# Sixteen full pages of a routed feed-forward are worked on between the norms and the routing of the last quarter of tokens

## The chip, the cores and the metric

The kernel runs on one core of a Trainium2 chip. The core has five engines with a queue of instructions each: TensorE (PE in the profile; PEld are its weight loads), VectorE (DVE), ScalarE (ACT), GpSimd (POOL) and SyncE (SP), which mostly issues transfers. Each engine works through its own instructions in the order in which the program gives them, and waits for semaphores where it needs what another engine or a transfer makes. The metric is device time in microseconds (us); lower is better. The runs of the kernel before took 815.91 us in the median (812.72, 815.91, 818.84).

## What is computed

The input x has 8 sequences of 256 tokens with 256 numbers each, 2,048 tokens, all in 32-bit floating point. One layer is computed:

```python
x = x + attention(layernorm(x))
x = x + ffn(layernorm(x))
```

The attention is differential: 16 heads with two sets of queries and keys of 8 numbers, two softmaxes, and their difference weighted by a scalar lambda, then a root-mean-square norm of each head's 16 numbers and a product with wo:

```python
attn = attn1 - lambda_full * attn2
rms = rsqrt(mean(attn * attn, axis=-1) + 1e-5)
attn = (attn * rms * subln_w * (1 - LAMBDA_INIT)).reshape(b, t, 256) @ wo.T
```

The feed-forward is a mixture of experts. A gate gives each token 32 logits; the four largest are chosen and weighted by a softmax over those four:

```python
logits = x @ gate_w.T
sel = top_k(sigmoid(logits), 4)
w = softmax(logits)[sel]; w = w / w.sum()
```

There are 32 large experts (256 to 96 to 256) and 16 small ones (256 to 128 to 256); two neighbouring large experts share a small one. Each token goes through its four large experts and the small ones that belong to them:

```python
a = silu(x @ Wg[e]) * (x @ Wu[e]) * w        # likewise with cWg, cWu of e // 2
y += a @ Wd[e]                               # likewise 0.05 * (a_small @ cWd[e // 2])
```

## The kernel before, in words

**Quarters and steps.** The tokens are worked on in four quarters of 512 (`NIT` = 4, index `it`). Attention of a quarter has four steps, one for each group of four heads, so there are sixteen steps `s`. Scores, exponentials, products with the values and the running maxima of the next step are interleaved by hand (`both`, `values`, `normalize`). What belongs to the end of a quarter (`epilogue`: norm of the heads, product with wo, layer norm, then `route`) is a Python generator that yields after each small group of instructions; `fill` takes one piece after another of it in between the attention of the next quarter. So the order on TensorE, ScalarE, VectorE and SP is that in which the program issues its instructions (`manual_schedule`, `MANUAL`), and Pool's order is left to the planner.

**Pages.** `route` (L543) gives each of a token's four choices a row in a page. A page (`pages` in device memory) has 128 rows of 304 numbers and belongs to one expert; a row holds the normed token, its 32 weights and its token number. When an expert's page is full, it gets the next free number. The state that goes from quarter to quarter is small: `held` (pages of each expert so far), `given` (pages given out, a running sum), `shift_of`, `count` and `chosen` (the expert of each page, one page per partition). The rows are written by indirect transfers of Pool, one for each choice and 128 tokens (L671, "puts"): 16 in a quarter.

**The last quarter.** No attention is left to hide its epilogue. It is cut into two halves of 256 tokens (`halves`, made at the end of the attention's block), which the loop under `with ExitStack() as last` (L848) takes in turns, one piece of each. The norms' roots (`rsqrt`, L249) are Ln and Exp on ScalarE with one refining step on VectorE. At the end of the second half's routing, `tables` (L688) makes for every page the offsets of its expert's weights (`table`, read into TensorE's registers) and the expert's number (`expert`). The gate and up weights of the small experts, `ws_sb`, are loaded at the start of this stretch in four transfers of 1 MB (L840), since they take the room of attention's buffers.

**The pages' work.** `run_tiles` works on 84 pages (`OFTEN`); up to 11 more follow if the routing gave out more. A page goes through five stages, which are staggered: `fetch` (L868: SP loads page i, seven pages ahead, eight buffers), `turn` (L872: token numbers and weights are copied or picked out on VectorE, two transposes on TensorE, the copy `xTe` on VectorE), `up` (L889: eight matrix products `gu` for gate and up of the large and the small expert, Silu on ScalarE, the product `act` on VectorE), `turn_act` (L921: two transposes, two copies `aTe`) and `down` (L930: the products `dn`, their scaling by the weight on ScalarE, and an indirect transfer on Pool that adds the rows to a sum in device memory, L943). Even pages add to one sum, odd pages to another, and two adds to one sum never overlap. The first sum also holds the attention's result of each quarter (L536). At the end both sums are read, added and written out.

Of the kernel before, what the change touches and what calls it, by code (L numbers as in the profile page):

```python
# [33 lines left out]
OFTEN = 84  # L34
RW = 304
# [4 lines left out]
def kernel(  # L40
# [171 lines left out]
    )  # L212

# [17 lines left out]
    with actx:  # L231
# [17 lines left out]
        def rsqrt(dst, v, tag):  # L249

            y = r2.tile(list(v.shape), F32, tag=f"{tag[0]}ry", name=f"ry_{tag}")
            nc.scalar.activation(y, v, AF.Ln)
            nc.scalar.activation(y, y, AF.Exp, scale=-0.5)
            yield "any"
            t = r2.tile(list(v.shape), F32, tag=f"{tag[0]}rt", name=f"rt_{tag}")
            nc.vector.scalar_tensor_tensor(t, y, -0.5, y, ALU.mult, ALU.mult)
            nc.vector.tensor_tensor(t, t, v, ALU.mult)
            nc.vector.scalar_tensor_tensor(dst, t, 1.5, y, ALU.add, ALU.mult)

        def layernorm_T(src, dst, tag, rows=None, n=NA):  # L260
# [12 lines left out]
            yield from rsqrt(rs, ve, f"n{tag}")  # L273
# [225 lines left out]
        def epilogue(it, a0=0, n=NA):  # L499
# [19 lines left out]
            yield from rsqrt(rms, ms, f"h{tag}")  # L519
# [16 lines left out]
            nc.sync.dma_start(out=sums_dram[0][ts].rearrange("(a p) e -> p a e", p=P), in_=xt)  # L536
            x2 = turned("x2T", tag, n, hidden)
            yield from layernorm_T(xt, x2, f"f{tag}", rowsrc[:, a0 : a0 + n, 0:E], n)
# [4 lines left out]
        def route(it, x2, a0, n):  # L543
# [13 lines left out]
            if a0 == 0:  # L557
                t = choice[it] = {
                    name: r1.tile([P, NA, w], F32, tag=name, name=f"{name}_{it}")
                    for name, w in (  # L560
                        ("lg", NE), ("top", 8), ("ex", NE), ("eq", NE), ("key", 8), ("mask", NE),
                        ("slots", NE), ("slot", 8), ("wsum", 1),
# [51 lines left out]
            slots, slot = t["slots"], t["slot"]  # L614
            nc.vector.tensor_copy(slots, pos.rearrange("p (a e) -> p a e", e=NE))
            nc.vector.tensor_scalar(whole, whole, 7, None, ALU.logical_shift_right)
# [50 lines left out]
            for a in range(n):  # L667
                if it + 1 < NIT:
                    yield "any"
                for k4 in range(TOPK):  # L670
# [9 lines left out]
                    tc.add_to_no_dep_group("puts", put.ins)  # L680
                if it + 1 < NIT:
                    yield "wait"
            if m + n == NIT * NA:
                tables()
# [3 lines left out]
        def tables():  # L688

            tiles = e1.tile([1, 1], I32)  # L690
            nc.vector.tensor_copy(tiles, given[0:1, (NIT + 1) % 2, NE - 1 : NE])
            found["tiles"] = tiles
            whose = e1.tile([P, 2], I32)
            nc.vector.tensor_copy(whose[:, 1:2], chosen)
            nc.vector.tensor_scalar(whose[:, 0:1], whose[:, 1:2], NE - 1, None, ALU.bitwise_and)
            nc.vector.tensor_scalar(whose[:, 1:2], whose[:, 0:1], 1, None, ALU.logical_shift_right)
            et = e1.tile([P, 5], F32)
            nc.vector.tensor_copy(et[:, 0:1], whose[:, 0:1])
            for i, (j, size) in enumerate(((0, INTER), (1, P), (0, E), (1, E))):
                nc.vector.tensor_scalar(  # L700
                    et[:, 1 + i : 2 + i], whose[:, j : j + 1], float(size), None, ALU.mult
                )
            rows = one("rows")
            for i in range(4):
                nc.tensor.transpose(
                    rows[0:1, i * P : (i + 1) * P], et[:, 1 + i : 2 + i], ident
                )
            table = e1.tile([1, P, 4], I32)
            nc.vector.tensor_copy(
                table.rearrange("p t i -> p i t"),  # L710
                rows[0:1, 0 : 4 * P].rearrange("p (i t) -> p i t", t=P),
            )

            diag = e1.tile([P, P], F32)
            nc.vector.tensor_scalar(diag, ident, et[:, 0:1], None, ALU.mult)
            by_row = one("by_row")[:, 0:P]
            nc.tensor.matmul(by_row, lhsT=ones, rhs=diag, start=True, stop=True)
            expert = e1.tile([P, P], F32)
            nc.vector.tensor_copy(expert, by_row)
            found["tables"] = (table, expert)  # L720
# [117 lines left out]
    for kc in range(2):  # L838
        for i, w in enumerate((cwg, cwu)):
            nc.sync.dma_start(out=ws_sb[:, kc, i, :], in_=w[kc * P : (kc + 1) * P, :])  # L840
    iota = e1.tile([P, P], F32)
    nc.gpsimd.iota(
        iota, [[1, P]], base=0, channel_multiplier=0, allow_small_or_imprecise_dtypes=True
    )
# [3 lines left out]
    with ExitStack() as last, tc.manual_schedule(engines=MANUAL):  # L848
        del psum["big"]
        psum_pools(last, "last", 0, 8)  # L850

        for _ in range(4):
            next(halves[0])
        while halves:
            for g in list(halves):
                if next(g, None) is None:
                    halves.remove(g)
            fill("any")
        while side:
            fill("pe", "any")  # L860

    table, expert = found["tables"]
    ps_e = xctx.enter_context(tc.tile_pool(name="ps_e", bufs=2, space=bass.MemoryType.PSUM))

    with tc.manual_schedule(engines={mybir.EngineType.PE, mybir.EngineType.Pool}):
        regs, xg, xT, act, aT, weight, token = {}, {}, {}, {}, {}, {}, {}

        def fetch(i):  # L868
            xg[i] = e2.tile([P, RW], F32, tag="xg", name=f"xg_{i}", bufs=8)
            nc.sync.dma_start(out=xg[i], in_=pages[i])  # L870

        def turn(i):  # L872

            token[i] = e2.tile([P, 1], I32, tag="token", name=f"token_{i}", bufs=10)
            nc.vector.tensor_copy(token[i], xg[i][:, RT : RT + 1].bitcast(I32))  # L875
# [170 lines left out]
```

## Time and profile before

| what | value |
| --- | --- |
| runs | 812.72, 815.91, 818.84 us |
| the profiled execution | 821.01 us, of which the span from first to last instruction is 818.8 |
| TensorE busy | 662.6 us (81% of the span), mean granted clock 0.882 |
| VectorE, ScalarE, Pool busy | 378.8, 276.8, 246.9 us |
| transfers | 83.58 MB, 102 GB/s in the mean |
| last attention product (TensorE) | ends near 470 us |
| first page fetched (SP) | 527.75 us |
| first and last add to the sums (Pool) | 542.45 and 790.56 us |

All positions are in us from the start of the span. A row of a timeline gives the start, the duration, the engine, the line of the kernel, the operation, what it writes and reads, how many instructions are merged, and in brackets how long the engine had been idle and what ended that. A row of the waits gives who waited for whom, the us in total, how often, and the longest. "issue" in the chain is time in which an engine waited for nothing that the profile shows, "remote" a wait for an event that it can't assign. The page's slices give busy shares in tenths, 9 for 90% or more.

### The profile page before, as it was taken

The page shows a single profiled execution, that of the slowest core. Times are in us where ns is not written, and L with a number is a line of the kernel's source. Part 1 is how long each engine was busy: PE and PEld are TensorE (multiplying, and loading weights), DVE is VectorE, ACT ScalarE, POOL GpSimd, SP SyncE. Part 2 cuts the span into 40 slices and gives each one's busy share as a digit, 9 for nine tenths or more (in the row PEclk, how much of TensorE's full clock was granted, in tenths as well). Part 3 has the DMA queues.
Part 4 walks back from the last instruction along what each step waited for, and adds up shares of the span by engine and source line. Part 5 has one row for each costly group of instructions (what it writes and reads, how often), then busy time and mean ns, then how long its engine had stood idle before and what let it go on. Part 6 is the DMA issues. An engine that isn't in the chain of part 4 may idle for free.

```text
span 818.8 us, 12293 instructions
## 1 busy us (share of the span) xinstructions
PE 662.6 (81%) x4108; PEld 428.5 (52%) x4108; DVE 378.8 (46%) x1111; ACT 276.8 (34%) x539; POOL 246.9 (30%) x246
## 2 busy tenths in 40 slices
PE   7789989899659998688886652199999999999930
PEld 6445434445224554233442242098888888888830
DVE  2274556555726666435654146243443344344312
ACT  2025545545215553234443311033223322332320
POOL 5000111111171110622105202524555455455540
PEclk7889999999868998878979665589999999999975
DMA  3107071714232334211461150445555555555347
GB/s 105 30 15 245 10 231 48 231 41 124 77 114 55 119 96 131 87 43 44 102 157 69 53 232 31 135 102 99 94 95 99 93 94 97 97 90 98 45 55 299
DMA packets 62512, 83.58 MB, mean 102 GB/s; under 512 B 8049, under 2 KB 54257, under 8 KB 61937
## 3 DMA queue, kind: packets, MB, share of 16 engines
q1 hardware_dynamic: 45488, 58.50, 23.5%
q0 software_dynamic: 15168, 20.98, 15.3%
q10 hardware_dynamic: 1792, 3.28, 1.3%
q8 instruction: 37, 0.61, 0.3%
q14 instruction: 27, 0.21, 0.1%
HBM read 36.23 MB, written 42.31 MB: 96 GB/s over the span
## 4 chain that ended last, share of the span: by engine, by line
PE 41%; DMA 22%; DVE 17%; issue 9%; ACT 5%; another core or an unknown queue 4%; SPq 1%; ACTq 0%; POOL 0%; DVEq 0%
DMA sums<-ye,token 18%; PE sm L411 9%; PE sc L395 8%; PE pv L448 7%; DVE mp L424 6%; PE gu L909 2%; PE wo L315 2%; PE po L467 2%; PE qps L352 2%; ACT ye L942 2%; PE vps L315 2%; DMA y<-sums 2%; DVE xTe L886 1%; DVE act L919 1%
## 5 line engine op out<-in xcount | busy, mean ns | idle before, releaser
L424 DVE TENSOR_REDUCE mp<-sm 128x4 f32<-128x1024 f32 x128 | 156.0, 1223 | 145.3 <-PE sm L411 127.2
L411 PE MATMUL sm<-kb,qT 32*128 32x512 f32 x512 | 159.5, 720 | 42.1 <-DVE mp L424 34.7
L421 ACT ACTIVATE pt<-sc 128x1024 f32<-128x1024 f32 x128 | 130.5, 1023 | 185.6 <-PE sm L411 149.5
L943 POOL DMA_INDIRECT sums<-ye,token x84 | 131.1, 1561 | 134.8 <-ACT act L918 106.8
L395 PE MATMUL sc<-qa,kb 32*128 32x256 f32 x1024 | 159.6, 437 | 11.4 <-ACT pt L421 6.5
L395 PEld LDWEIGHTS sc<-qa,kb 32*128 32x128 f32 x1024 | 88.0, 201 | 56.8 <-issue 32.9
L486 POOL TENSOR_SCALAR on<-on,nlam 128x128 f32<-128x128 f32 x28 | 17.0, 606 | 309.7 <-DVE on L474 286.9
L909 PE MATMUL gu<-ws_sb,xTe 128*128 x336 | 87.4, 383 | 0.0
L671 POOL DMA_INDIRECT pages<-rowsrc,index x64 | 62.7, 980 | 66.2 <-issue 52.8
L875 DVE COPY token<-xg 128x1 int32<-128x1 int32 x84 | 12.9, 154 | 150.7 <-DMA sums<-ye,token 136.3
L448 PE MATMUL pv<-pt,vaug 128*32 128x512 f32 x512 | 76.8, 671 | 5.5 <-ACT oT L457 5.5
L927 ACT ACTIVATE aTe<-at 128x128 f32<-128x128 f32 x84 | 23.3, 278 | 164.2 <-DVE aTe L926 164.1
L411 PEld LDWEIGHTS sm<-kb,qT 32*128 32x128 f32 x512 | 42.7, 204 | 61.0 <-DVE mp L424 50.2
L909 PE MATMUL gu<-wl_sb,xTe 128*128 x336 | 70.6, 333 | 0.6 <-DMA xg<-pages 0.6
L909 PEld LDWEIGHTS gu<-ws_sb,xTe 128*128 128x128 f32 x336 | 62.5, 193 | 4.5
L909 PEld LDWEIGHTS gu<-wl_sb,xTe 128*128 128x128 f32 x336 | 57.5, 192 | 8.6 <-issue 2.9
L933 PE MATMUL dn<-wdl_sb,aTe 96*128 x168 | 53.6, 401 | 0.0
L937 PE MATMUL dn<-wds_sb,aTe 128*128 x168 | 50.1, 379 | 0.0
L884 PE MATMUL xt<-ident,xg 128*128 128x128 f32 x168 | 32.7, 278 | 12.5 <-DMA xg<-pages 12.5
L942 ACT ACTIVATE ye<-dn,weight 128x256 f32<-128x256 f32 x84 | 39.4, 469 | 1.1 <-PE dn L937 1.0
L886 DVE COPY xTe<-xt 128x256 f32<-128x256 f32 x84 | 35.3, 420 | 8.2 <-PE xt L884 8.0
L448 PEld LDWEIGHTS pv<-pt,vaug 128*32 128x32 f32 x512 | 10.7, 113 | 50.7 <-issue 42.6
(178 smaller groups left out, 781.1 us busy)
## 6 DMA issues: line engine op xcount, KB each, us to landing
pages<-free SPq DMA_DIRECT2D x31, 456.0 KB
xg<-pages SPq DMA_DIRECT2D x84, 152.0 KB
wl_sb<-in_wg_dram SPq DMA_DIRECT2D x8, 384.0 KB
wl_sb<-in_wu_dram SPq DMA_DIRECT2D x8, 384.0 KB
wdl_sb<-in_wd_dram SPq DMA_DIRECT2D x8, 384.0 KB
x<-in_x_dram SPq DMA_DIRECT2D x4, 512.0 KB
kb<-packk SPq DMA_DIRECT2D x128, 16.0 KB
sums<-zero SPq DMA_DIRECT2D x8, 256.0 KB
```

What stands on the lines that cost most here:

```text
L395: nc.tensor.matmul(sc[:, j, h * 256 : h * 256 + 256], lhsT=kb[s][rows, h, c * P : (c + 1) * P], rhs=qa[s][rows, c // 2 * 256 : c // 2 * 25 ...
L411: nc.tensor.matmul(sm[:, j, :], lhsT=qT[m][rows, a * P : (a + 1) * P], rhs=kb[m][rows, :, ks], start=True, stop=True,)
L421: nc.scalar.activation(pt, sc, AF.Exp, scale=SM_SCALE)
L424: nc.vector.tensor_reduce(mps[m % 2][:, a, 2 * mp : 2 * mp + 2, 2 * D : 2 * D + 2], sm.rearrange("p j (s k) -> p j s k", s=2), AX.X, ALU.max,)
L448: nc.tensor.matmul(pv[s][32 * j : 32 * j + 32, :], lhsT=st_it[it][1][:, c, 4 * g + j, :], rhs=pts[(s, c, j // 2)][:, j % 2, :], start=(c % ...
L671: put = nc.gpsimd.indirect_dma_start(pages.rearrange("r s w -> (r s) w"), bass.IndirectOffsetOnAxis(ap=index[:, a, k4 : k4 + 1], axis=0), ...
L886: nc.vector.tensor_copy(xT[i], ps)
L909: nc.tensor.matmul(ps[:, :, cols], lhsT=xT[i][:, kc, :], rhs=w[:, kc, :, bass.ds(first, n)], start=(kc == 0), stop=(kc == 1),)
L933: nc.tensor.matmul(ps, lhsT=aT[i][0:INTER, 0], rhs=wdl[0:INTER, bass.ds(large, E)], start=True, stop=False,)
L937: nc.tensor.matmul(ps, lhsT=aT[i][:, 1], rhs=wds[:, bass.ds(small, E)], start=False, stop=True,)
L942: nc.scalar.activation(y, ps, AF.Copy, scale=weight.pop(i))
L943: nc.gpsimd.indirect_dma_start(sums_dram[i % 2], bass.IndirectOffsetOnAxis(ap=token.pop(i), axis=0), y, None, compute_op=ALU.add, oob_is_e ...
```

## The change

The quarters, the attention and the pages' work on a single page stay as they are. Changed is which pages are worked on when:

- After the routing of the third quarter, `full_first` marks the pages that are full by then (all of an expert's pages but its last, unless that one is full to the end). Ranks among the marked pages are found by a product with the triangular matrix `upper`; the first 16 (`FULL`) are put in order by a product with a one-hot matrix (`in_order`). No row of them is free for the last quarter, and none of their tokens is from it, so the program is told that their loads and adds don't depend on the last quarter's puts and stores.
- In the last quarter's loop each piece of a half is followed by two pieces of `run_tiles(0, FULL)`, which has become a generator; 16 pages are interleaved with the two halves there. The stretch has its own banks of PSUM: two for the transposes, two for gate and up, one for the down product, and three for the halves (before, the halves had eight).
- `rest_after` takes the place of `tables`: it orders the remaining pages in the same way after the last routing, and the pages from 16 on follow in the old place.
- Since the order of the pages is known only on chip, each `fetch` reads the page's number into a register of SP first.
- The roots of the last quarter (`by_bits`) are made on VectorE from the number's bits and three refining steps, eleven instructions, without Ln and Exp. ScalarE still has the routing's Exp, between the pages' Silu. For the first 16 pages ScalarE makes both `aTe` copies.
- `ws_sb` is loaded in 16 transfers of 256 KB, four columns of experts at a time; `iota` moves to the start of the kernel.

On Pool, the order in which the program is built is: adds of pages 0 to 10, the 8 puts of the first half, adds of pages 11 and 12, the 8 puts of the second half, adds of pages 13 to 15, then the rest. On SP the store of the first half's rows stands behind the 16 loads of `ws_sb` and ahead of page 0, that of the second half behind page 11.

The diff, cut to its core:

```diff
+FULL = 16
...
-        def rsqrt(dst, v, tag):
+        def rsqrt(dst, v, tag, by_bits=False):
             y = r2.tile(list(v.shape), F32, tag=f"{tag[0]}ry", name=f"ry_{tag}")
+            if by_bits:
+                t = r2.tile(list(v.shape), F32, tag=f"{tag[0]}rt", name=f"rt_{tag}")
+                nc.vector.tensor_scalar(
+                    t.bitcast(I32), v.bitcast(I32), 1, None, ALU.logical_shift_right
+                )
+                nc.vector.tensor_scalar(
+                    y.bitcast(I32), t.bitcast(I32), -1.0, float(0x5F3759DF), ALU.mult, ALU.add
+                )
+                for i in range(3):
+                    nc.vector.scalar_tensor_tensor(t, y, -0.5, y, ALU.mult, ALU.mult)
+                    nc.vector.tensor_tensor(t, t, v, ALU.mult)
+                    nc.vector.scalar_tensor_tensor(
+                        dst if i == 2 else y, t, 1.5, y, ALU.add, ALU.mult
+                    )
+                return
...
-            yield from rsqrt(rms, ms, f"h{tag}")
+            yield from rsqrt(rms, ms, f"h{tag}", not hidden)
...
-            yield from layernorm_T(xt, x2, f"f{tag}", rowsrc[:, a0 : a0 + n, 0:E], n)
+            yield from layernorm_T(xt, x2, f"f{tag}", rowsrc[:, a0 : a0 + n, 0:E], n, not hidden)
...
+            if it + 2 == NIT:
+                yield from full_first(k + 1, chosen_by)
             if m + n == NIT * NA:
-                tables()
+                yield "any"
+                yield from rest_after()
...
+        def in_order(pool, name, et, flags, rank, n):
+            at = pool.tile([P, n], F32, name=f"at_{name}")
+            nc.vector.tensor_scalar(at, iota[:, 0:n], rank, flags, ALU.is_equal, ALU.mult)
+            by = pool.tile([P, n], F32, name=f"by_{name}")
+            nc.vector.tensor_scalar(by, at, et[:, 0:1], None, ALU.mult)
+            yield "pe"
+            rows = one(f"rows_{name}")
+            for i in range(5):
+                nc.tensor.matmul(
+                    rows[0:1, i * n : (i + 1) * n], lhsT=et[:, 1 + i : 2 + i], rhs=at,
+                    start=True, stop=True,
+                )
...
+            yield "pe"
+            ps = one(f"expert_{name}")
+            nc.tensor.matmul(ps[:, 0:n], lhsT=ones, rhs=by, start=True, stop=True)
...
+        def rank_of(pool, name, flags):
+            ps = one(f"rank_{name}")
+            nc.tensor.matmul(ps[:, 0:1], lhsT=upper, rhs=flags, start=True, stop=True)
+            rank = pool.tile([P, 1], F32, name=f"rank_{name}")
+            nc.vector.tensor_copy(rank, ps[:, 0:1])
+            return rank
+
+        def full_first(k, chosen_by):
+            yield "any"
...
+            full = r1.tile([P, 1], F32, name="full")
+            nc.vector.tensor_scalar(full, given[:, k % 2, NE - 1 : NE], tok[:, 0:1], None, ALU.is_gt)
+            nc.vector.tensor_tensor(full, full, part, ALU.subtract)
+            et = whose_pages(r1, "full")
+            yield "pe"
+            rank = rank_of(r1, "full", full)
+            nc.vector.scalar_tensor_tensor(
+                in_full, rank, float(FULL), full, ALU.is_lt, ALU.mult
+            )
+            yield from in_order(r1, "full", et, in_full, rank, FULL)
...
+    def load_small(c):
+        cols = slice(c * P, (c + 4) * P)
+        for kc in range(2):
+            for i, w in enumerate((cwg, cwu)):
+                nc.sync.dma_start(out=ws_sb[:, kc, i, cols], in_=w[kc * P : (kc + 1) * P, cols])
...
+    def fetch(i):
+        table, j, first = place(i)
+        _, (at,) = nc.values_load_multi_w_load_instructions(
+            table[0:1, j, 4:5], engines={mybir.EngineType.SP},
...
+        load = nc.sync.dma_start(
+            out=xg[i], in_=pages[bass.ds(at, 1)].rearrange("one s w -> (one s) w")
+        )
+        if first:
+            tc.declare_no_dep(
+                load.ins, group="last puts", reason="no row of a full page is free"
+            )
+            tc.add_to_no_dep_group("full pages", load.ins)
...
-            nc.vector.tensor_copy(aT[i][0:INTER, 0], ps[0:INTER, 0])
+        (nc.scalar.copy if i < FULL else nc.vector.tensor_copy)(aT[i][0:INTER, 0], ps[0:INTER, 0])
...
-    with ExitStack() as last, tc.manual_schedule(engines=MANUAL):
+    with ExitStack() as gap, tc.manual_schedule(engines=MANUAL):
         del psum["big"]
-        psum_pools(last, "last", 0, 8)
+        psum["tiles"] = gap.enter_context(
+            tc.tile_pool(name="ps_full", bufs=2, space=bass.MemoryType.PSUM)
+        )
+        psum["tr"], psum["dn"] = 2, 1
+        psum_pools(gap, "gap", 0, 3)
+        load_small(0)
+        tiles = run_tiles(0, FULL)
         for _ in range(4):
             next(halves[0])
+        for c in range(4, NC_SMALL, 4):
+            load_small(c)
         while halves:
             for g in list(halves):
                 if next(g, None) is None:
                     halves.remove(g)
+                for _ in range(2):
+                    next(tiles, None)
             fill("any")
+        for _ in tiles:
+            pass
...
-        run_tiles(0, OFTEN)
+        for _ in run_tiles(FULL, OFTEN):
+            pass
```

## The prediction

> **What bounds the kernel now.** I read the page's slices first, then the chain of work that ended last, then the timeline of one engine after another around the stretch that the change fills. Three rows of the slices (20.5 us each; TensorE busy, its granted clock, DMA, in tenths):
>
> ```profile
> PE   7789989899659998688886652199999999999930
> PEclk7889999999868998878979665589999999999975
> DMA  3107071714232334211461150445555555555347
> ```
>
> Attention fills the left, the pages' work the right; between them TensorE falls to 2 and 1 tenths at half clock. The chain in order of time and Pool's and SP's timelines say what is there:
>
> ```profile
> 489.80 37.95 issue
> 529.55 2.24 DMA xg<-pages
> ...
> 764.26 3.89 DMA sums<-ye,token
> ```
>
> ```profile
> 505.73 0.99 POOL L671 DMA_INDIRECT pages<-rowsrc,index  x1 [35.65 <-issue]
> 507.02 0.96 POOL L671 DMA_INDIRECT pages<-rowsrc,index  x1 [0.30 <-issue]
> ...
> 525.26 0.96 POOL L671 DMA_INDIRECT pages<-rowsrc,index  x1 [0.30 <-issue]
> ```
>
> ```profile
> 472.44 0.35 SPq L840 DMA_DIRECT2D ws_sb<-in_cwg_dram  x1
> ...
> 527.75 2.23 SPq L870 DMA_DIRECT2D xg<-pages  x5
> ```
>
> From 470 to 527.75 the last quarter is normed and routed, and its 16 puts, 1.27 us apart on Pool, end it: the first page is fetched 2.49 us after the last put starts. Then 84 pages follow, and their rate is Pool's:
>
> ```profile
> 678.83 1.56 POOL L943 DMA_INDIRECT sums<-ye,token  x1 [1.11 <-ACT act L918]
> 682.30 1.56 POOL L943 DMA_INDIRECT sums<-ye,token  x1 [1.92 <-ACT act L918]
> 684.96 1.56 POOL L943 DMA_INDIRECT sums<-ye,token  x1 [1.10 <-ACT act L918]
> ```
>
> An add waits for the add before it on the same of two sums (678.83 to 684.96: 6.1 us a pair). First add 542.45, last 790.56, so 2.99 us a page, and 28.2 us after the last one. TensorE alone would need 2.82: from 540 to 560, before the adds hold it back, its gate and up groups start 2.82 us apart.
>
> **The change, part by part.**
>
> *Sixteen pages leave the last phase*: 16 x 2.99 = 47.8 us. There are always sixteen: 1,536 tokens times 4 rows are 6,144, 32 experts can leave at most 32 x 127 of them in short pages, so 2,080 remain, 17 pages at least. What counts is how late the 17th page is fetched against 527.75, since its fetch still waits for the last put. Break-even is a fetch at 575.5.
>
> *When the early pages start.* The small experts' weights are still loaded at 472.4, now in 16 pieces with rows of 2 KB instead of 8. The row of before moved 4.2 MB at 422 to 434 GB/s; the nearest row with shorter ones, wds_sb with 1 KB, 348. So 9.7 to 12 us; I take 10.5, landed at 485. Half 0's root is now 11 dependent VectorE steps of 0.22 (2.4 us) instead of two table steps and three: x is ready about 1.6 us later, at 482, SP stores it and only then issues page 0's fetch (it stands behind that store), which takes 2.2 us as at 529.9 and comes in behind the weights. Transposes and copy follow, and gate and up start near 488.
>
> *The rounds.* The order on all engines is fixed: one page a round, a step of each half in between. TensorE from the first gate and up to dn of page 10: 6.4 us to the third at the cold clock (531.77 to 538.17 in the row), 2.6 to the first dn, ten pages at 2.82, and the routing's own steps between, at half their cold time (a wo 3.5 to 1.75, a set of transposes 1.08 to 0.54, lg, pos): 6.7. From 488 that is 531.9, if it never waits. It does wait, for VectorE:
>
> ```profile
> 680.09 0.15 DVE L875 COPY token<-xg 128x1 int32<-128x1 int32 x1 [2.27 <-DMA sums<-ye,token]
> 680.38 0.42 DVE L886 COPY xTe<-xt 128x256 f32<-128x256 f32 x1
> 680.71 0.38 DVE L919 TENSOR_TENSOR act<-act,gu 128x224 f32<-128x224 f32 x1
> 681.01 0.28 DVE L926 COPY aTe<-at 96x128 f32<-96x128 f32 x1
> ```
>
> A page costs VectorE 1.0 us there (the aTe copy goes to ScalarE for early pages). Between two pages now stand whole blocks of the routing. Behind them are queued the copy of the next page's transpose and its product, and TensorE stops once two pages are short. Two roots of 2.4 and 2.3 us in one round cost it 3.6; half 1's second root 1.1; the index block of 1.7 about 1. The fourth place is ScalarE, where Silu of the next page stands behind the routing's Exp, which waits for VectorE, and behind two table loads:
>
> ```profile
> 535.28 1.28 ACT L918 ACT_TABLE_LOAD   x1 [33.50 <-PE gu L909]
> 536.57 0.36 ACT L918 ACTIVATE act<-gu 128x224 f32<-128x224 f32 x1
> ```
>
> The two Exp now cost four more loads. By this row 4 x 1.28 = 5.1 us, of which 2.1 reach TensorE in the second Exp's round (the first is covered by VectorE's root). The Trainium skill, "ScalarE: Activation LUTs", section "What ACT_TABLE_LOAD costs", counts a drain of about 1.38 us more, 2.66 a switch: 10.6 in sum, and up to 5.5 us later. Here Silu starts 1.29 us after the load began, so I take the row. Waits in sum 7.8: dn of page 10 at 539.7.
>
> *Pool.* The last quarter's puts stand behind the adds in Pool's order: eleven adds, 8 puts of half 0, two adds, 8 puts of half 1, three adds. The eleventh add is issued 1.5 us after its dn, at 541.2, and takes 1.86 with its gap: 543.0. Half 0's rows are ready before that (541). 8 x 1.27 to 553.2; two adds to 556.9; the last put starts 7 x 1.27 later, at 565.8; the 17th fetch at 568.3. That is 40.5 us later than 527.75. Half 1's rows, ready near 550.5, are covered by 6 us of Pool's own queue, and the three last adds by the next pages' start-up of about 14 us.
>
> *Finding the pages* puts three small products and some 20 VectorE steps of 0.15 to 0.25 us into attention's last step, each product waiting for VectorE on the only bank of its kind. VectorE is idle there, but this is the stretch with the waits
>
> ```profile
> DVE r L473 <- remote: 17.5, 1, 17.5
> ACT pt L421 <- remote: 11.2, 3, 6.6
> ```
>
> (437 to 462, while 16 puts run): signals from TensorE reach the other engines microseconds late. Bounds: 0, if the chain waits anyway, to 10 (three trips of some 5 us, less 5 in hand); I take 2. The same lateness may meet the puts in the gap: 0 to 12, Pool's 6 us in hand taken off; I take 2.5, nearer to the last quarter's own puts, beside which VectorE ran on without such a wait.
>
> *Each fetch* now first loads the page's number into a register on SP. No row shows SP doing it. TensorE loads four such values a page and was busy 20.00 of 20 us from 540 to 560, so they hide there; the skill, "Runtime: NRT & Kernel Launch", section "Instruction fetch mechanics", states about 200 ns a register, 1.3 us for several. With SP's issue of 0.45 (five in 2.23) that is 0.65 to 1.75 us, under 2.99, and fetches run seven pages ahead. Cost: 1 us before the 17th page, against 1.3 saved because Silu's table is already there. The tables of the rest take the place of the old ones (4.4 us on VectorE), covered by the puts.
>
> *Sum*: -47.8 + 40.5 + 2 + 2.5 + 1 - 1.3 = -3.1. The profiled execution took 821.0 (span 818.8), so 817.9; it lies 5.1 above the median of the runs, 815.9, so **813**.
>
> **Rivals.** *The lookahead of two pages covers VectorE's blocks.* For it: VectorE is busy 5.8 of 12 and 7.3 of 10 us in the old gap, mostly small steps. Then half 0's puts wait for nothing but its own rows, near 532, and end at 542.4; adds and half 1's puts bring the fetch to 557.6, a delay of 29.9: -17.9, **798**. Against it: the blocks stand ahead of the copies in VectorE's order.
>
> *Signals come late whenever Pool puts* (the slower one). Three bursts of 16 puts in attention have these "remote" waits, from the fifth to eighth put on, and put 4 to 15 us each on the chain (33 us, 4% of the span, stand there as an unknown queue); in the old gap nothing depended on TensorE by then, now pages do. Finding the pages costs 5, the two bursts of 8 cost 12 beyond Pool's cover: -47.8 + 40.5 + 17 = +9.7, **826**. It decides once the 17th fetch is later than 575.5. Against: the adds of the last phase cause no such wait.
>
> *SP becomes the bound*: if the register load takes 2.8 us, each page costs 3.3 instead of 2.99, 68 pages +20: about **833**. Against it: TensorE's hidden loads.
>
> **How the numbers follow.** Forecast 0.42, better cover 0.27, late signals 0.25, SP 0.06. One per cent is about what the runs of this kernel (812.7 to 818.8) can tell from no change; its edges are 807.8 and 824.1. The forecast's own range is 804 to 822: a quarter of it lies beneath 807.8 (0.10), little above 824 (0.04). Faster: 0.10 + 0.25 = 0.35; slower: 0.18 of the late signals, 0.06, 0.04 = 0.28; the rest 0.37. The outer cases' own spread is some 8 us, so leaving a tenth at each end gives 798 to 829.
>
> **What would show it.** Right: adds to the sums from about 498; first puts of the last quarter near 543, the last near 566, the 17th fetch near 568 and about 2.99 us a page from there; TensorE at full clock from 495 to 545 with pauses before xt after the root blocks; five table loads. Better cover: dn of page 10 before 533. Late signals: "remote" waits among the pages' copies and Silu at 543 to 567. SP: fetches in the last phase spaced by SP and xt waiting for them. The forecast is wrong if the early pages start much after 488, or if attention's end moves by more than 3 us.

## The result, and the profile after

The changed kernel takes 812.25 us in the median of 20 runs (806.64 to 817.90), the kernel before 817.08 in 20 runs beside it (812.72 to 821.21): a ratio of 0.9947, 95% interval 0.9925 to 0.9969, so 2.5 to 6.1 us less. That is within one per cent. Its profiled execution has a span of 810.5 us against 818.8, at a granted clock of 0.894 against 0.882.

The same three rows of slices (20.3 us each; TensorE busy, its granted clock, DMA, in tenths):

```profile
PE   7878989899649998687875638983799999999940
PEclk9799999999879998879996658995799999999985
DMA  3116080704122334213442082434555655655347
```

The trough is split in two. Before the early pages there is one slice of 3, and after them another: between 540 and 570 us TensorE is busy 13.4 of 30 us. Pool's timeline (start, duration, idle before it and what ended that) shows the order that the prediction laid out, eleven adds, 8 puts, two adds, 8 puts:

```profile
536.34 1.55 POOL L1039 DMA_INDIRECT sums<-ye,token  x1 [2.18 <-DVE rowsrc L694]
538.20 1.00 POOL L706 DMA_INDIRECT pages<-rowsrc,index  x1 [0.31 <-issue]
...
547.13 0.96 POOL L706 DMA_INDIRECT pages<-rowsrc,index  x1 [0.31 <-issue]
...
552.19 1.00 POOL L706 DMA_INDIRECT pages<-rowsrc,index  x1 [0.30 <-issue]
...
561.12 0.96 POOL L706 DMA_INDIRECT pages<-rowsrc,index  x1 [0.30 <-issue]
```

SP's queue has the weights' first piece, page 0's fetch and the 17th page's fetch:

```profile
467.14 0.35 SPq L938 DMA_DIRECT2D ws_sb<-in_cwg_dram  x1
...
478.67 14.18 SPq L959 DMA_DIRECT2D xg<-pages  x12
...
568.44 30.50 SPq L959 DMA_DIRECT2D xg<-pages  x19
```

The 17th fetch goes out 7.32 us after the last put's start. Before the change the first fetch followed the last put by 2.49. What came last is in the chain of waits (start, us, what), and in TensorE's and VectorE's timelines:

```profile
545.37 5.68 another core or an unknown queue
551.43 1.04 another core or an unknown queue
...
559.12 7.75 another core or an unknown queue
566.87 0.84 DVE table_rest L760
```

```profile
562.93 1.48 PE L755 MATMUL rows_rest<-at_rest,et_rest 128*1 128x79 f32 x10
...
566.85 0.85 DVE L760 CAST table_rest<-rows_rest 1x395 int32<-1x395 f32 x1 [7.73 <-remote]
```

The products for the table of the remaining pages end on TensorE at 564.41, and VectorE starts the copy that waits for them 2.44 us later. SP reads its page numbers from that table, so not the last put but the table set the fetch.

The profiled pair, cut at the same events:

| stretch, us | before | after |
| --- | --- | --- |
| start to the third quarter's first put | 437.7 | 428.5 |
| to the small experts' first load | 34.8 | 38.7 |
| to the first fetch after the last puts | 55.3 | 101.3 |
| to the first add of those pages | 14.7 | 15.1 |
| adds that follow, first to last | 248.1 (83 x 2.989) | 199.1 (67 x 2.971) |
| to the end of the span | 28.3 | 27.9 |

In this pair the stretch that the change touches, from the third puts on, is 0.9 us longer (381.2 to 382.1), and the 8.3 us less of the span are attention's 9.2 ahead of it. Of these 9.2, 3.3 already lie ahead of ScalarE's first copy of an attention result (67.24 and 63.92), far from the change. In the medians 4.8 us were gained; the profiled execution of before, 821.01, lies 3.9 above its median, that of after at its own. One profile of each can't divide the gain: in the five profiles of changed kernels on what looks like the same kind of chip, the third puts began between 428.4 and 434.5.

### The profile page after: what moved, and what is told of

Same layout as the page of the kernel before. It is cut to its first block, busy times and chain, and to the rows that moved or that the text cites. A ratio compares the mean times of both kernels' runs of the same rounds, so it can differ in the third digit from the quotient of the medians.

```text
span 810.5 us, 12637 instructions
## 1 busy us (share of the span) xinstructions
PE 655.8 (81%) x4130; PEld 424.8 (52%) x4130; DVE 383.2 (47%) x1154; ACT 285.1 (35%) x551; POOL 246.4 (30%) x247
## 4 chain that ended last, share of the span: by engine, by line
PE 59%; DVE 15%; DMA 11%; another core or an unknown queue 5%; issue 4%; SPq 3%; ACT 3%; ACTq 0%; POOL 0%; DVEq 0%
PE gu L1005 13%; PE sc L420 8%; PE sm L436 8%; PE pv L473 7%; DVE mp L449 6%; DMA sums<-ye,token 5%; PE dn L1029 3%; PE dn L1033 3%; PE po L492 2%; SPq L399 2%; DMA y<-sums 2%; PE xt L980 2%; PE qps L377 2%; PE wo L340 2%
## 5 line engine op out<-in xcount | busy, mean ns | idle before, releaser
L436 PE MATMUL sm<-kb,qT 32*128 32x512 f32 x512 | 152.4, 691 | 42.7 <-DVE mp L449 31.5
L420 PE MATMUL sc<-qa,kb 32*128 32x256 f32 x1024 | 153.1, 428 | 5.0 <-DVE mp L449 3.5
L420 PEld LDWEIGHTS sc<-qa,kb 32*128 32x128 f32 x1024 | 85.1, 198 | 46.1 <-issue 30.2
L1005 PE MATMUL gu<-wl_sb,xTe 128*128 x336 | 75.3, 348 | 4.4 <-issue 1.7
L1014 ACT ACTIVATE act<-gu 128x224 f32<-128x224 f32 x84 | 30.1, 358 | 41.1 <-PE gu L1005 34.7
L1015 DVE TENSOR_TENSOR act<-act,gu 128x224 f32<-128x224 f32 x84 | 31.9, 380 | 24.5 <-ACT act L1014 18.9
```

The lines of the kernel that those rows point to most:

```text
L420: nc.tensor.matmul(sc[:, j, h * 256 : h * 256 + 256], lhsT=kb[s][rows, h, c * P : (c + 1) * P], rhs=qa[s][rows, c // 2 * 256 : c // 2 * 25 ...
L436: nc.tensor.matmul(sm[:, j, :], lhsT=qT[m][rows, a * P : (a + 1) * P], rhs=kb[m][rows, :, ks], start=True, stop=True,)
L1005: nc.tensor.matmul(ps[:, :, cols], lhsT=xT[i][:, kc, :], rhs=w[:, kc, :, bass.ds(first, n)], start=(kc == 0), stop=(kc == 1),)
```

## The experiments

The experiments ran on three chips, each beside the kernel before. That kernel took 815 us on the chip of full24, full8, roots_scalar and no_last_puts, 775 on that of roots_one_round, find_early, spread24 and join24, and 774 on that of before_hand, after_hand, spread16 and join16; beside the changed kernel it had taken 817. So the results are ratios to the kernel before on the same chip. On the two faster chips the unedited after was not run, so what is said of after there rests on its ratio of 0.9947 carrying over.

**Eight more pages, eight fewer.** The edits of full24 and full8 (the narrower `iota`, in full24 alone, makes room for larger tables):

```diff
-FULL = 16
+FULL = 24        # full8: FULL = 8
-    iota = const.tile([P, P], F32)
+    iota = const.tile([P, NTILE - FULL], F32)
```

> 24 instead of 16 pages ahead of the last puts (this input has 33 full ones by then; 17 are guaranteed for any). My theory: between 545 and 577 TensorE stands still for want of pages (busy 13.4 us of 30 from 540 to 570), since page 17 waits for the last put, the rest's table and a start-up of 15 us; eight more pages fill that time. Dn of page 10, the puts and the adds between them stay where they are (last put near 561); then Pool issues adds 13 to 23 one after the other and reaches the 24th near 583; the rest's first add follows near 590 instead of 607 for the same page. That is 13 to 19 us off 812: 793 to 799. Rival (signals from TensorE come late whenever Pool puts): the extra pages crawl between 545 and 565 as pages 13 to 15 do, some 5 us each, the first add of the rest comes near 600, and 5 to 8 us are gained: 804 to 807. Second rival (a page costs the same wherever it is worked on): no change, 810 to 814.

Measured: 808.77 us against 814.77, ratio 0.9936 (0.9909 to 0.9963). The theory failed. By the ratio it is no faster than after (0.9947), as the second rival had it; the trace shows what the first rival described, and a border besides. The last put is where it was (561.12), but the extra pages were hardly worked on while Pool put. First the timeline of TensorE and ScalarE, then Pool's:

```profile
557.70 1.91 PE L1005 MATMUL gu<-ws_sb,xTe 128*128 x4
...
565.42 0.36 ACT L1014 ACTIVATE act<-gu 128x224 f32<-128x224 f32 x1 [8.10 <-PE gu L1005]
```

```profile
593.98 1.55 POOL L1039 DMA_INDIRECT sums<-ye,token  x1 [1.13 <-ACT ye L1038]
605.11 1.55 POOL L1039 DMA_INDIRECT sums<-ye,token  x1 [9.57 <-ACT ye L1038]
```

ScalarE took up a gate-and-up group that ended at 559.61 only at 565.42; TensorE was long at its next products by then (the next group starts at 559.54). And between page 23's add and page 24's lie 11.1 us, since the pages' pipeline is drained and filled again at the border of the two phases.

> Eight instead of 16 pages ahead of the last puts. My theory: a page in the gap costs less than the 2.97 us that it costs after it. Without the last eight, half 0's rows are ready near 530 and half 1's before its puts' turn; the sixteen puts run one after the other without adds between them, the last starts near 549, the first later fetch is near 552, and 76 pages at 2.97 follow: 6 us longer than after, 818 (815 to 821), about the kernel before. Rival (what was gained comes from fewer pages in the last phase alone and the last puts keep their place at 561): 812 + 24 = 836. Second rival (pages in the gap cost as much as outside it): 812.

Measured: 820.63, ratio 1.0068 (1.0041 to 1.0095). The later fetch started at 553.02 (552 expected), 84.8 us after the weights' first load where after has 101.3. Eight pages in the gap so cost 16.5 us there, 2.06 each, and save 2.97 each: the gain is that difference. The direction of the theory held, its size was low: by the ratios full8 is 1.2 per cent, some 10 us, slower than after, where 6 (3 to 9) were expected; in its profile the 76 later pages went at 3.02 us each. Eight pages ahead of the puts even lose against the kernel before: what the new stretch costs once, they don't earn back.

**Roots back on ScalarE.** In roots_scalar `by_bits` is left off at both roots; roots_one_round also takes out the stop between Exp and VectorE's step in the last quarter:

```diff
-            yield from rsqrt(rms, ms, f"h{tag}", not hidden)
+            yield from rsqrt(rms, ms, f"h{tag}")
...
             nc.scalar.activation(y, y, AF.Exp, scale=-0.5)
-            yield "any"
+            if "3_" not in tag:        # roots_one_round alone
+                yield "any"
```

> The four roots of the last quarter go back to ScalarE (Ln, Exp and one step on VectorE), everything else as in after. My theory: each of the four then changes ScalarE's table twice among the pages' Silu, up to eight loads of 1.28 us more, and VectorE is 4 x 1.6 us shorter; TensorE, which is two pages ahead, loses 3 to 6 us up to dn of page 10 and the time goes up by as much: 815 to 818. Rival (VectorE's root blocks are what TensorE waits for, 7.8 us in my sum, and ScalarE's loads hide in the lookahead): dn of page 10 comes 3 to 5 us earlier and the time is 807 to 810. No difference, 811 to 813.5, if both are hidden behind TensorE's own steps.

Measured: 817.94, ratio 1.0024 (0.9995 to 1.0052), by the ratios some 6 us more than after's 0.9947. The first theory held in size. But Pool's order now had 13 adds ahead of half 0's puts, so the loads could not be the whole of it.

> Roots of the last quarter on ScalarE as in roots_scalar, but without the stop that stood between Exp and VectorE's step, so that each root takes one round of the order as in after. roots_scalar had put 13 adds ahead of half 0's puts instead of 11: two rounds more. My theory now: of the 6 us that it cost against after, some 4 are these two rounds of nearly 3 us each (less what TensorE gains in them) and 2 the table loads; so this kernel loses 1 to 3 us against after: 0.996 to 0.999 of before, puts of half 0 behind 11 or 12 adds. Rival (table loads among the pages' Silu are the whole cost): as roots_scalar, 1.002 of before. Second rival (VectorE's root blocks cost TensorE what I summed, 7.8 us, and the loads cost nothing): 0.990 or less.

Measured: 771.36 against 775.06, ratio 0.9959 (0.9931 to 0.9988), with 11 adds ahead of the puts. From the first gate and up to the eleventh add it took 55.3 us, in after 51.8, in find_early on the same chip 49.5. The ratio lies at the lower edge of what was expected, and both rivals' figures (1.002, and 0.990 or less) lie outside its interval. ScalarE's timeline shows one root:

```profile
449.46 0.76 ACT L1015 ACTIVATE act<-gu 128x224 f32<-128x224 f32 x2
450.25 1.28 ACT L277 ACT_TABLE_LOAD   x1
451.54 0.23 ACT L277 ACTIVATE ry_h<-ms 128x32 f32<-128x32 f32 x1
451.79 1.28 ACT L278 ACT_TABLE_LOAD   x1
453.08 0.23 ACT L278 ACTIVATE ry_h<-ry_h 128x32 f32<-128x32 f32 x1
...
453.65 1.28 ACT L1015 ACT_TABLE_LOAD   x1
454.95 0.36 ACT L1015 ACTIVATE act<-gu 128x224 f32<-128x224 f32 x1
```

A root between two Silu cost three loads, 13 in the gap instead of 5 (8 x 1.28 = 10.2 us of ScalarE), and the rounds got 3.5 to 5.8 us longer. The Trainium skill ("ScalarE: Activation LUTs", section "Table sets: the hidden batching unit") has Ln and Exp share one set and one load. In before the trace agrees until the pages' first Silu: the kernel itself has the set with both loaded at 2.87 us, and the roots' 14 Ln and 14 Exp follow without a load. Between the Silu here each had its own. The drain beside a load, which the prediction quotes, is not seen either: work follows 1.29 to 1.30 us after a load of 1.28 begins. How the 6 us of roots_scalar divide between loads and rounds can't be told closely, since the two kernels ran on different chips.

**No puts of the second half.**

```diff
-                for k4 in range(TOPK):
+                for k4 in range(TOPK if a0 == 0 else 0):
```

> Leaves out the eight puts of the last quarter's second half, so those rows are never worked on (the pages' number stays). Only the trace counts. My theory: the table of the rest comes late (2.44 us from the end of its products on TensorE to VectorE's copy, 5.5 us for the copy of the ranks, 5.2 for act) because Pool issues puts at that time. Without them these waits fall below 1 us each, the table is there near 553 to 556, and the 17th fetch starts there. Rival (the table is late because its products stand in TensorE's order among the pages, behind act and dn): the waits stay 2 to 5 us and the table comes near 560 or later.

Theory and rival were both half right. Half 0's puts ended at 551.66; until 555.34 ScalarE waited on TensorE as in after, and then the lateness was gone:

```profile
555.34 0.36 ACT L1014 ACTIVATE act<-gu 128x224 f32<-128x224 f32 x1 [5.24 <-remote]
...
561.60 1.48 PE L755 MATMUL rows_rest<-at_rest,et_rest 128*1 128x79 f32 x10
...
563.11 0.85 DVE L760 CAST table_rest<-rows_rest 1x395 int32<-1x395 f32 x1 [4.88 <-PE rows_rest L755]
```

VectorE's copy starts 0.03 us after the products' end at 563.08, where after needed 2.44. But the table was still there only at 563.96: its products stood in TensorE's order behind the last pages' dn, which the lateness had held up. The fetch started at 564.70, 25.6 us after dn of page 10 instead of 32.9.

**Finding the full pages ahead of the third puts.**

```diff
+            if it + 2 == NIT:
+                yield from full_first(k + 1, chosen_by)
             for a in range(n):
                 if it + 1 < NIT:
                     yield "any"
...
-            if it + 2 == NIT:
-                yield from full_first(k + 1, chosen_by)
```

> Finding the full pages stands ahead of the third quarter's puts instead of behind their emission, all else as in after. In after, from the first put of the third quarter to the small experts' first load it took 38.7 us, 34.8 before the change. My theory: the three round trips TensorE to VectorE during the puts cost the 3.9 us, since they come late there; ahead of the puts they are quick, and the load starts 2 to 4 us earlier relative to attention: 808.5 to 811 where after has 812. Rival (VectorE and TensorE have no room there either, or the puts themselves now come later and the end of attention waits on something else): no change within 1 us, or up to 3 us slower.

Measured: 773.23 against 775.06, ratio 0.9979 (0.9955 to 1.0003); as the rival had it. TensorE, in the midst of attention's scores, now waits for VectorE's steps:

```profile
407.39 0.56 PE L774 MATMUL rank_full<-full,upper 128*128 128x1 f32 x2 [5.81 <-DVE who_full L734]
```

The weights' load came 25.3 us after the third puts' start, where after_hand, with the finding in after's place, has 20.4. The theory itself was not put to the test: no signal is late on this chip (the last section), so there was nothing to avoid.

**Puts handed out in pairs, one stream of pages.** spread24 is full24 with VectorE writing the indices of two puts at a time, a round apart; join24 also lets all 84 pages run as one stream, with VectorE's and ScalarE's order by hand to the end:

```diff
+                    if it + 1 == NIT and k4 % 2 == 0:
+                        nc.vector.tensor_scalar(
+                            index[:, a, k4 : k4 + 2], slot[:, a, k4 : k4 + 2], -1.0, None, ALU.add
+                        )
                     put = nc.gpsimd.indirect_dma_start(
...
+                        if k4 % 2:
+                            next(rest, None)          # a step of rest_after
+                            yield "any"
...
-        tiles = run_tiles(0, FULL)                    # join24 alone
+        tiles = run_tiles(0, OFTEN)
```

> As full24, with the last quarter's sixteen puts handed out two at a time, a round of the order apart (VectorE writes their indices two columns at a time), so that adds stand between them on Pool: 4, 2, 2, 6 and 2 puts instead of 8 and 8; the rest's tables are worked out beside them. In full24 signals from TensorE reached ScalarE and VectorE up to 8 us late while eight puts ran one behind the other and for 3.4 us after, and pages 16 to 23 were not worked on in that time. Theory: the lateness comes from unbroken puts; broken up, TensorE goes on at near 3 us a page, page 23's add comes near 584 instead of 594, and the rest follows as much earlier: 797 to 802, 0.98 to 0.985 of before. Rival (any put makes signals late, or Pool as a whole when it has no idle time): page 23's add stays at 590 to 596 and the time at 806 to 810.

> spread24, and the pages run as one stream: the later pages follow on page 23 without draining the pipeline (same PSUM pools, VectorE's and ScalarE's order by hand to the end). In full24 the first later add came 11.1 us after page 23's, 8 us more than a page's time. Theory: these 8 us go: 8 less than spread24. Rival (the order by hand and one bank for dn cost the 60 later pages more than 0.13 us each): no gain or a loss against spread24.

Measured: spread24 763.82 against 775.06, ratio 0.9857 (0.9828 to 0.9886); join24 744.57, ratio 0.9594 (0.9567 to 0.9621). spread24's page 23 was added 91.0 us after page 0, full24's 97.8 (on a chip with late signals). join24 gained 19 us on spread24 where 8 were expected. Pool's timeline of spread24, then of join24, at the border of pages 23 and 24:

```profile
545.40 1.55 POOL L1046 DMA_INDIRECT sums<-ye,token  x1 [1.14 <-ACT ye L1045]
556.59 1.55 POOL L1046 DMA_INDIRECT sums<-ye,token  x1 [9.64 <-ACT ye L1045]
```

```profile
545.06 1.55 POOL L1047 DMA_INDIRECT sums<-ye,token  x1 [1.11 <-DMA xg<-pages]
547.21 1.55 POOL L1047 DMA_INDIRECT sums<-ye,token  x1 [0.60 <-ACT ye L1046]
```

The border took 2.2 us instead of 11.2, which is the 9 us expected; the other 10 are the 59 later pages, 2.78 us apart instead of 2.95. Pool had the same adds, so its adds don't set the rate.

**VectorE's and ScalarE's order by hand.** One line, in before (before_hand) and in after (after_hand):

```diff
-    with tc.manual_schedule(engines={mybir.EngineType.PE, mybir.EngineType.Pool}):
+    with tc.manual_schedule(engines=MANUAL | {mybir.EngineType.Pool}):
```

> The kernel before, with one line changed: in the pages' last phase VectorE's and ScalarE's instructions keep the order in which the code emits them, instead of one that the scheduler finds (TensorE and Pool kept it already). My prediction called the rate of 2.99 us a page Pool's. New theory from join24 (2.82 us a page with the same adds on Pool): the scheduler moves the copy of a later page's token ahead on VectorE until it waits for an add to land (its ten buffers), and behind it stand the copy of xT and the product; that wait sets the rate, Pool doesn't. By hand each token is copied eight pages after its buffer's add was issued, so 83 pages at 2.82 instead of 2.99: 14 us or 1.7 per cent less, 0.983 of before (0.980 to 0.986). Rival (the rate is Pool's, an add waiting for the add before it on the same sums): no change, 0.998 to 1.002.

> After, with the same one line changed for the 68 later pages. Theory: 67 x 0.15 = 10 us less than after, 0.982 of before (0.979 to 0.985); so the change's gain is measured against a phase in which each page moved is worth 2.82 instead of 2.99: against before_hand the sixteen pages gain nothing (0.998 to 1.003). Rival (Pool's rate): as after, 0.9947.

Measured against 773.54: before_hand 759.75, ratio 0.9804 (0.9768 to 0.9840); after_hand 756.14, ratio 0.9761 (0.9727 to 0.9796). The waits of the last phase (who for whom, us in total, times, longest), first of before from 600 to 780 us, then of before_hand from 560 to 700:

```profile
ACT aTe L927 <- DVE aTe L926: 123.5, 60, 2.6
DVE token L875 <- DMA sums<-ye,token: 102.8, 56, 2.4
POOL sums L943 <- ACT act L918: 84.8, 58, 1.9
```

```profile
DVE act L919 <- ACT act L918: 83.4, 50, 1.7
ACT aTe L927 <- DVE aTe L926: 63.8, 50, 1.4
POOL sums L943 <- ACT ye L942: 59.1, 48, 1.9
```

VectorE's wait for an add is gone. The chain of before, from one add to the next but one, shows how that wait set the rate:

```profile
678.83 3.64 DMA sums<-ye,token
...
682.75 0.07 DVE token L875
...
683.75 0.21 DVE aTe L926
...
684.22 0.47 ACT ye L942
...
684.96 3.63 DMA sums<-ye,token
```

These are the add of page 45, the token of page 55, `aTe` of page 48, and `ye` and the add of page 47. In before's order a token is copied four pages early. That of page 55 takes the buffer of page 45, one of ten, and so waits for page 45's add to land; behind it on VectorE stands `aTe` of page 48; ScalarE's half of that copy waits for VectorE's, and behind it on ScalarE stands the scaling of page 47. So two pages had to fit into an add's landing and these steps, which took 684.96 - 678.83 = 6.1 us. By hand the token of page 54 stands directly ahead of `xTe` of page 54 (635.32 in before_hand), 15.1 us or some five pages after the start of page 44's add (620.26), and waits for nothing. TensorE was then busy 160.00 of 160.00 us from 540 to 700, at 2.82 us a page; in before it shows 157.68 for the same stretch, so its busy time alone would not have told. The one line changes both engines' order; which of the two would have been enough was not tried.

The last part of after_hand's expectation missed: against before_hand it still gains, ratio 0.995 by the medians (a resampling of the six runs of each gives 0.992 to 0.998). Its timelines of TensorE, VectorE, Pool and SP show what was left out:

```profile
507.98 0.84 PE L755 MATMUL rows_rest<-at_rest,et_rest 128*1 128x79 f32 x10
508.87 0.85 DVE L760 CAST table_rest<-rows_rest 1x395 int32<-1x395 f32 x1 [2.28 <-PE rows_rest L755]
...
519.29 0.96 POOL L706 DMA_INDIRECT pages<-rowsrc,index  x1 [0.30 <-issue]
521.96 13.52 SPq L959 DMA_DIRECT2D xg<-pages  x13
```

On this chip nothing is late: the table is ready 9.6 us before the last put starts, and the fetch follows that put by 2.67 us.

**Pairs and one stream with 16 pages.** spread16 and join16 are the two kernels above with `FULL` = 16; in join16 the stream stops until the last puts are handed out.

> After (16 pages), with the last quarter's puts handed out two at a time and the rest's tables worked out beside them, as in spread24. Pool's order is 4 puts, add, 2, add, 2, two adds, 2, add, 6. In after the table of the rest was copied 7.7 us late and the 17th fetch went out 7.3 us after the last put's start instead of 2.5. Theory (late signals beside unbroken puts): the table is there before the last put, the fetch follows it by 2.5 us; but three more adds now stand before the last put (5.6 us), so the fetch comes within 1 us of where it came: 0.993 to 0.996, as after. Rival (late signals whatever the order): the fetch comes 5 us later than in after: 1.000.

> join24 with 16 pages ahead of the last puts, the number that any input of this size has. The stream of pages stops at the 14th until the last puts are handed out, its tail follows with the 17th page. Theory: it gains the 10 us of VectorE's order and loses the ten pages' worth of work that join24 does while Pool puts: about as after_hand, 0.978 to 0.986. Rival (the joined stream is what gained, whatever the number): near join24, 0.960 to 0.968.

Measured: spread16 774.68, ratio 1.0009 (0.9983 to 1.0034): the last puts were later, as expected (68.8 us after the first add, in after_hand 63.2), and the fetch followed the last by 2.7 us as the theory had it; but there was no lateness to win back on this chip, and the rest's first add came 7.2 us later than after_hand's by the same count. So the time missed the theory's 0.993 to 0.996. It is the rival's figure, but not for the rival's reason, a late fetch. join16: 756.53, ratio 0.9767 (0.9733 to 0.9801), as after_hand and as its theory. The stream alone gains nothing without pages to work on while Pool puts.

join24 is the fastest of all. It takes for granted that 24 pages are full by then, which holds for this input (33 are); any input has 17.

## Why the prediction was right, and where it wasn't

The time came out, 813 predicted and 812.25 measured, and Pool's order, the early start and the rounds as described. Two steps behind it were wrong, and part of the agreement is luck. One of the prediction's own signs of being wrong appeared: the weights' first load, at attention's end, came 5.3 us earlier (472.44 to 467.14), where more than 3 was to count against it. The 17th fetch, at 568.44 where near 568 was predicted, is right only because the way from that load to it was longer by as much. Terms in us, from the profile of after and from the pair after_hand and before_hand, where no signal is late:

| term | predicted | after | after_hand |
| --- | --- | --- | --- |
| 16 pages fewer in the last phase | -47.8 | -49.0 | -44.5 |
| finding the pages | 2 | 3.9 | 1.9 |
| weights' load to the first gate and up | 15.6 | 17.4 | 17.6 |
| to dn of page 10 | 51.7 | 51.0 | 49.4 |
| to the last put's start | 26.1 | 25.6 | 25.5 |
| to the 17th fetch | 6.0 | 7.3 | 2.7 |

**When the early pages start**: 1.8 us off. Page 0's fetch landed 4.5 us after its issue at 478.67, behind the weights in the same queues; I had taken 2.2. (The prediction's own sum has a slip here: 472.4 + 10.5 is 482.9, not 485.) **The rounds**: within 1 us. TensorE stood idle for 5.3 us of them (7.8 predicted), 3.6 of these for `xTe` from VectorE, and was busy for 45.8 (43.9 predicted); the five table loads are there at 1.28 each. **Pool**: half 0's puts began 2.6 us after dn of page 10 (3.3 predicted). **The register load**: the first ten fetches on SP start 0.85 us apart (0.65 to 1.75 predicted, 0.47 before), so a load takes about 0.4 us, where the prediction had allowed 0.2 to 1.3. The 17th fetch shows next to none of it: 2.67 us after the last put in after_hand, 2.49 in before.

**Late signals**: the mechanism was right, the term too small, and it was put at the wrong place. I had it at the puts' own inputs, with 6 us of Pool's work in hand; it struck the table of the rest, which I had called "covered by the puts". Lateness took 7.3 - 2.7 = 4.6 us at the fetch (2.5 predicted), and finding the pages cost 3.9 instead of 1.9. The chain of waits has 14.5 us of late signals between 545 and 567, but most of that passed beside puts that had to run anyway; so most of the slow rival's 17 us did not come about.

**The rate of the last phase** is the step that failed: "their rate is Pool's". The 2.989 us a page were right as a number and stayed so in after (2.971), because the scheduler's order stayed; but VectorE's early token copy set them, by its wait for an add to land. The prediction read its 6.1 us a pair as an add waiting for the add before it on the same sum. The rows that it shows speak against that: at 680.09 the landing of page 44's add (started at 676.16) releases the token copy, and the next add to the same sum starts at 682.30, 2.2 us later. By hand a page is worth 2.80, and the change is still worth its 0.5 per cent there, since on that chip its fetch also comes earlier.

**The sum** came out closer than its parts. In the profiles of before and after the changed stretch gained nothing (+0.9 us); by the pair on the other chip it gained 2.7 (-44.5 + 40.4 + 1.9 - 0.5 for the start-up), and 2.0 came from third puts that began earlier (408.41 to 406.40). Why attention ended earlier in these pairs, and by how much it does in the mean, stays open. What the unedited after gains on a chip without late signals was not measured. An estimate: find_early's later pages are 2.96 us apart, after_hand's 2.80, so after_hand's 756.14 + 67 x 0.16 = 767, 0.991 of before, a gain of some 7 us.

## What to carry to other kernels

Work moved into a gap pays by the difference between what a step costs there and where it was (here 2.06 against 2.97 us a page), and the border it creates, a drained pipeline or a new table on the way, can cost more than the steps themselves. When a steady phase goes slower than its busiest engine does the same work elsewhere (here 2.99 us a page against 2.82), look for an instruction that a scheduler has moved ahead and that waits for a buffer: those behind it on the same engine pay for it. And compare only runs of one chip: here the same kernel took 815 us on one, 775 and 774 on two others.

## What was not expected of the hardware

In the profiles of before, after and the four kernels on the 815 us chip, ScalarE and VectorE took up TensorE's results late while Pool issued unbroken puts, and for 3.3 to 4.8 us after: the puts ended at 562.08 in full24 and in after, at 551.66 in no_last_puts, the last late steps started at 565.42, 566.85 and 555.34. The chain of before has 33 us in such waits (4.0% of the span), that of after 5.0%. Of the eight profiles on the two other chips none has such a wait. The text calls this late signals; the profile models the ends of TensorE's instructions, so whether the signal or its receiver was late isn't shown. The ends of two neighbouring attention steps around the first puts show the size, ScalarE's copies in before and in before_hand:

```profile
217.33 0.58 ACT L457 COPY oT<-pv 128x512 f32<-128x512 f32 x1
243.93 0.59 ACT L457 COPY oT<-pv 128x512 f32<-128x512 f32 x1 [3.18 <-remote]
```

```profile
215.28 0.58 ACT L457 COPY oT<-pv 128x512 f32<-128x512 f32 x1
230.35 0.58 ACT L457 COPY oT<-pv 128x512 f32<-128x512 f32 x1
```

That is 26.6 us against 15.1, with the same instructions. Each chip was used at one time only, so whether it is the chip or something else of that time isn't told apart, and the cause was not found. It also means that spread24's gain on full24 can't be given to the spreading: full24 ran where signals are late, spread24 where they aren't, and spread16 lost by spreading.
